# The last four rounds of a fused four-layer convolution in another order

## The chip, the cores and the metric

The kernel runs on one core of one Trainium2 chip. The metric is the device time of one execution in microseconds (us). TensorE (PE in the profile) multiplies matrices, VectorE (DVE), ScalarE (ACT) and GpSimd (POOL) work elementwise, and SyncE (SP) issues most of the transfers. Each engine takes its instructions in the order in which the program issues them to it.

## The reference

Each of 128 samples has 64 channels of 1024 positions. Four convolutions with three taps run one after the other, with weights that are modulated and normalised per sample; the second doubles the length and blurs, the fourth blurs and halves it. The input is added at the end.

```python
s = style @ mw.T + mb
weight = SCALE * w * s[:, None, :, None]
demod = lax.rsqrt(jnp.sum(weight * weight, axis=(2, 3)) + EPS)
weight = weight * demod[:, :, None, None]
...
for i, typ in enumerate(('same', 'upsample', 'same', 'downsample')):
    out = _layer(out, style, weights[i], biases[i], mod_w[i], mod_b[i], typ)
x = x + out
```

## The kernel before, in words

**What is multiplied.** The four layers of one sample are one linear map with nine taps of 64 by 64. The kernel works on quads of four samples, 32 quads in all (`q` counts from 0 to 31). For each quad TensorE first folds the layers: `stage1` (tile S), `stage2` (tile R) and `stage3` (tile Wf, in two parts), each followed by a scaled copy on ScalarE (`scaled_copy`, L361 for a copy on ScalarE). The nine taps stand in Wf as three groups a, b, c of three. Then the quad's samples, split into three planes by position modulo three, are convolved by five products instead of nine: products 0 and 4 use a and c as they are, products 1, 2 and 3 use combinations h1, h2, h3 of a, b, c (tile H).

**The work of one quad outside TensorE.**
- `combine_a` and `combine_b` (L601, L611) build h1, h3 and h2 on VectorE by `sum_of` (L595); `residual` (L587, L592) adds the identity to b.
- `in3` (L642), `in_g01` (L647), `in_g2` (L652) and `in04` (L667) make the combined planes on VectorE (tiles T and G); `in1` and `in2` (L657, L662) run on GpSimd for most quads and on VectorE for the last one.
- All five products run through `product` (L676; matmuls at L687). Products 3, 1, 2 and 0 use one pair of banks psA in that order, product 4 uses the pair Y. One group of a product is 8 matmul instructions, a whole product 24.
- Between the products the banks are read: `copy_m3` (L716, ScalarE, L719) after product 3, `sum1` (L724) after product 1, `sum2` (L733: first Y, then y at L738) after product 2. Product 1 adds into the banks that `copy_m3` reads, product 2 into those that `sum1` reads, product 0 into those that `sum2` reads, so each of them waits for the reader before it. Product 4 adds into Y and waits for the first half of `sum2`.
- `output` (L748; L756 on ScalarE, L758 on VectorE) scales a plane and adds the bias, `store` (L760) sends it to memory.

**The order.** Nothing is planned by a program: the loop at L1211 writes the order out by hand, and each engine keeps it. Round `q` holds the folding of quad `c = q + 2` (stages 2 and 3) and `s = q + 4` (stage 1), products 4 and 0 of quad `q`, and products 3, 1 and 2 of quad `n = q + 1`. On TensorE a middle round reads: stage2(c), product 4 of q, stage3(c, 0), product 3 of n, stage3(c, 1), product 0 of q group 0, product 1 of n with stage1(s) between its groups, product 0 of q groups 1 and 2 with the rest of stage1(s), product 2 of n. Rounds 28 and 29 have no stage 1 (s is 32 and more), and round 30 (L1245 to L1267) and round 31 (L1216 to L1228) have texts of their own. In round 29 VectorE also prepares quad 31: `combine_a(31)` with `sum1(30)` between its steps (L1330), `combine_b(31)`, and after `sum2(30)` its `in1` and `in2` (L1369 to L1372).

**Banks.** The psA of quads 0 to 30 come from a pool of two pairs (ps_conv). The psA of quad 31 comes at L1247 from ps_w, a pool of one pair of single banks that the folding stages use too; since these are two tiles, `copy_m3`, `sum1` and `sum2` of quad 31 work bank by bank, with two instructions each.

**The row ends** are computed apart: `slot(ends3, ...)` (L1308; matmuls at L924 into psE of ps_w, two copies at L779), `rest3` (L1014) and `rest3_bias` (L1026, and one transfer).

**EXTRA** (L1167 to L1198) hangs small steps of the scales and tables at places (round, place): place 0 before `in04(n)`, place 1 before `sum1(n)`, place 2 before product 2's second group. `var_newton` (L265, three VectorE instructions at L256 to L258) refines the inverse roots of layers i to j for quads 8 to 31; `table_C` (L305, GpSimd, L288) multiplies two of them for the R copies from quad 8 on; `small_rest` (L1159, L860 and L861) makes a bias vector on VectorE.

Of the kernel before, what the change touches and what calls it, by code (L numbers as in the profile page):

```python
# [50 lines left out]
ALU = mybir.AluOpType  # L51
# [12 lines left out]
def kernel(  # L64
# [12 lines left out]
    NQ = B // 4  # L77
# [187 lines left out]
    def var_newton(bs, ls=slice(0, NL)):  # L265

        newton(var[:, ls, bs], dm[:, ls, bs], nw[:, ls, bs])
# [37 lines left out]
    def table_C(bs, eng=nc_g):  # L305
        table(eng, tC, bs, slice(0, 2), slice(2, 4), dm[:, 1, bs], dm[:, 0, bs])

    def table_3(bs):
        table(nc_g, t3, bs, ALT, ODD, dm[:, 3, bs], var[:, 3, bs])
        table(nc_g, td, bs, slice(0, 2), slice(2, 4), dm[:, 3, bs], 1.0)  # L310
# [283 lines left out]
    def sum_of(out, x, f, y, op=ALU.add):  # L594
        nc_v.scalar_tensor_tensor(out, x, f, y, op0=ALU.mult, op1=op)  # L595
# [2 lines left out]
        W, H_ = Wq[q]  # L598
        return *(W[:, :, i] for i in range(K)), *(H_[:, i] for i in range(3))

    def combine_a(q, between=None):  # L601

        chain.pop(q)
        a, b, c, h1, h2, h3 = taps(q)
        sum_of(h1, c, -2.0, a)
        residual(q)
        if between:
            between()
        sum_of(h3, h1, 1.0 / 6.0, b)

    def combine_b(q):  # L611

        a, b, c, h1, h2, h3 = taps(q)
        sum_of(h2, c, -0.5, a)
        sum_of(h1, b, -3.0, h2, ALU.subtract)
        sum_of(h2, h2, -1.0 / 3.0, b)


    NJ = NB + 2
# [81 lines left out]
    def parts(q):  # L701

        if isinstance(A[q], list):
            return [(slice(s, s + 1), A[q][s][:, None, :NB]) for s in range(2)]
        return [(slice(0, 2), A[q][:, :, :NB])]
# [6 lines left out]
    def conv3(q, pool=None):  # L712
        A[q] = unit(pool, f"psA{q}") if pool else ps_conv.tile([P, 2, 512], F32, tag="u", name=f"psA{q}")
        product(q, 3, banks(q))
# [15 lines left out]
    def conv2(q, *groups):  # L730
        product(q, 2, banks(q), groups or range(K))

    def sum2(q):  # L733
        m3 = m3c.pop(q)
        for s, a in parts(q):
            sum_of(Y[:, s, :NB], m3[:, s], 3.0, a)
        for s, a in parts(q):
            nc_v.tensor_sub(y1w[q][:, s], y1w[q][:, s], a)  # L738

    def conv4(q, *groups):  # L740
# [31 lines left out]
    def slot(matmuls, n, ps, wide=WIDE):  # L772

        matmuls(ps)
        turn[0] ^= 1
        r = raw[turn[0]]
        for i in range(2):
            src = ps[i][:, : HB * max(n, wide)].rearrange("c (b j) -> c b j", b=HB)
            nc_a.copy(r[:, i, : HB * n].rearrange("c (b j) -> c b j", b=HB), src[:, :, :n])  # L779
# [29 lines left out]
    def vector_Da(bs):  # L809
        nc_g.tensor_mul(Da[:, bs], sc[:, 3, bs], dm[:, 2, bs])  # L810
# [5 lines left out]
    def vector_c0(bs):  # L816
        with_bias(c0f, dm[:, 1], 0, bs)
# [4 lines left out]
    def vector_c2(bs):  # L822
        with_bias(c2f, sc[:, 3], 2, bs)
# [335 lines left out]
    def small_rest(q):  # L1159
        l, bs = SMALL[q]  # L1160
        const_rest(l, bs, high(bs.stop - bs.start))

    def layers(i, j):
        return REST, slice(i, j)
# [6 lines left out]
        (3, 0): lambda: var_newton(*layers(2, 3)),  # L1171
        (3, 1): lambda: (table_A(REST, dm[:, 2, REST]), small_rest(3)),
        (3, 2): lambda: (table_b(PART[1]), table_0(REST), vector_b1(REST), tap_differences()),
        (4, 0): lambda: var_newton(*layers(0, 2)),
        (4, 2): lambda: (vector_c0(REST), table_C(REST)),
        (5, 0): lambda: var_newton(*layers(3, 4)),
        (5, 1): lambda: small_rest(5),
        (5, 2): lambda: (table_3(REST), vector_c2(REST), vector_Da(REST)),
        (6, 1): lambda: small_rest(6),
        (7, 1): lambda: small_rest(7),  # L1180
        (7, 2): lambda: (table_b(REST), zeros()),
# [11 lines left out]
        (22, 0): lambda: (blur_side(0, 0), blur_side(1, 0)),  # L1193
        (23, 0): lambda: (blur_side(0, 1), blur_side(1, 1)),
        (24, 0): lambda: (blur_side(0, 2), blur_side(1, 2)),
        (28, 2): rest3,
        (29, 0): rest3_bias,
    }  # L1198

    def extra(*at):  # L1200
# [10 lines left out]
    for q in range(NQ):  # L1211
# [32 lines left out]

        if n == NQ - 1:  # L1245

            conv3(n, ps_w)  # L1247
            copy_m3(n)
            conv4(q, 0, 1)
            for i in range(2):  # L1250
                output(q, 1, i)
            conv1(n)
            sum1(n)
            conv4(q, 2)
            for i in range(2):
                output(q, 2, i)
                store(q, i, slice(1, K))
            in04(n, PAIR[0])
            in04(n, PAIR[1])
            conv0(q, 0)  # L1260
            conv2(n)
            conv0(q, 1, 2)
            sum2(n)
            for i in range(2):
                output(q, 0, i)
                store(q, i, slice(0, 1))
            continue  # L1267
# [36 lines left out]
            stage3(c, 1)  # L1304
        if q in SLOTS:
            slot(*SLOTS[q], Y_banks)
        if q == NQ - 4:
            slot(ends3, 3, unit(ps_w, "psE"), 3)  # L1308
        conv0(q, 0)
        if q in SMALL:  # L1310
            small(q)
        if q == 2:
# [2 lines left out]
        if twice:  # L1315
            stage1(s - 1)
        elif s < NQ:
            stage1_a(s)
        conv1(n, 1, 2)
        for i in range(2):  # L1320
            output(q, 1, i)
# [2 lines left out]
        if q > 1:  # L1324
            in_g2(c)
            if not late(q):
                load(c + NX)
        extra(q, 1)
        if n == NQ - 2:
            combine_a(n + 1, lambda: sum1(n))  # L1330
            combine_b(n + 1)
        else:
            sum1(n)
        if q == 0:
            in3(c)
        if q == 1:
            in_g01(c)
        conv0(q, 1)
        if twice:
            stage1_a(s)  # L1340
        elif s < NQ:
# [25 lines left out]
            scale3(s + 2)  # L1367
        conv2(n, 1, 2)
        if n == NQ - 2:  # L1369
            sum2(n)  # L1370
            in1(n + 1, nc_v)
            in2(n + 1, nc_v)  # L1372
        for i in range(2):
            store(q, i, slice(0, 1 if late(q) else K))
# [78 lines left out]
```

## Time and profile before

| | |
|---|---|
| median of 3 runs | 482.5 us (482.35, 482.5, 485.54) |
| the profiled execution | 481.36 us, of which its span is 479.6 us |
| PE busy | 471.5 us (98%) |
| DVE busy | 397.8 us (83%) |
| ACT busy | 304.3 us (63%) |
| POOL busy | 137.8 us (29%) |
| granted TensorE clock | 0.998 |

Times in the views are us from the start of the span. In a timeline row stand the start, the time from the first start to the last end, the engine, the line, the operation, the written and the read tile, the number of instructions, and in brackets how long the engine had been idle and what released it. Ends of matmuls are modelled: the next matmul starts about 0.2 us before the end of the one before it, so that the distance between two starts says more than the length of a row.

### The profile page before, as it was taken

The numbers are of one execution on the slowest core, as the hardware profiler recorded it, in microseconds if no ns is written. First come the engines' busy times: TensorE is split into PE (matmuls) and PEld (weight loads), VectorE is DVE, ScalarE is ACT, GpSimd is POOL, SyncE is SP. The second block draws the span as 40 slices with busy tenths as digits, with TensorE's granted clock in tenths as the row PEclk, the third lists the DMA queues.
The fourth block names the chain that finished last, engine by engine and source line by source line (L and its number), as shares of the span: only waits on it lengthen the run. The fifth ranks groups of instructions, "written<-read, shape, count | busy, mean of one in ns | idle before, by whom it ended". The sixth has DMA issues, their size and how long they took to land. (4 is left out here: it accounts for less than half of the span.)

```text
span 479.6 us, 25784 instructions
## 1 busy us (share of the span) xinstructions
PE 471.5 (98%) x11592; PEld 356.3 (74%) x11592; DVE 397.8 (83%) x660; ACT 304.3 (63%) x621; POOL 137.8 (29%) x171
## 2 busy tenths in 40 slices
PE   8999999999999999999999999999999999999996
PEld 7977788878788877777777777666777777777753
DVE  4899998798898988878868988758988887787784
ACT  5465666666666766767667666667666666765442
POOL 3433132644314333303333212333113333322100
PEclk9999999999999999999999999999999999999999
DMA  7116365245444535443445544444543445554314
GB/s 248 55 56 208 105 203 182 91 150 178 151 151 123 169 126 180 149 150 111 160 150 160 168 149 142 135 143 155 166 150 123 154 152 180 162 164 150 106 62 176
DMA packets 50494, 70.65 MB, mean 147 GB/s; under 512 B 5648, under 2 KB 47312, under 8 KB 50384
## 3 DMA queue, kind: packets, MB, share of 16 engines
q1 hardware_dynamic: 49792, 68.32, 44.3%
q8 instruction: 91, 1.49, 1.3%
q10 hardware_dynamic: 592, 0.69, 0.4%
q14 instruction: 19, 0.16, 0.1%
HBM read 35.36 MB, written 33.62 MB: 144 GB/s over the span
## 5 line engine op out<-in xcount | busy, mean ns | idle before, releaser
L687 PE MATMUL psA<-T,H 64*64 64x340 f32 x2304 | 190.8, 446 | 1.2 <-DVE y L595 1.2
L687 PEld LDWEIGHTS psA<-T,H 64*64 64x64 f32 x2304 | 93.5, 133 | 52.9 <-issue 3.4
L446 POOL TENSOR_TENSOR S<-S 128x128 f32<-128x128 f32 x28 | 14.3, 511 | 268.8 <-ACT S L361 259.9
L595 DVE SCALAR_TENSOR_TENSOR G<-X 128x684 f32<-128x684 f32 (+1 forms) x65 | 76.5, 1212 | 0.0
L687 PE MATMUL psA<-T,Wf 64*64 64x340 f32 x768 | 74.0, 446 | 0.0
L361 ACT ACTIVATE R<-psR,tC 128x448 f32<-128x448 f32 x63 | 36.6, 631 | 42.4 <-PE psR L467 26.6
L361 ACT ACTIVATE Wf<-psW,t 128x384 f32<-128x384 f32 (+1 forms) x126 | 56.4, 498 | 11.1 <-PE psW L574 10.2
L687 PE MATMUL Y<-T,Wf 64*64 64x340 f32 x768 | 61.7, 446 | 0.1
L574 PE MATMUL psW<-R,w0s 64*64 64x128 f32 (+1 forms) x1536 | 61.7, 287 | 0.0
L574 PEld LDWEIGHTS psW<-R,w0s 64*64 64x64 f32 x1536 | 51.2, 133 | 6.9
L595 DVE SCALAR_TENSOR_TENSOR Y<-m,psA 128x680 f32<-128x680 f32 (+1 forms) x33 | 28.0, 849 | 33.3 <-PE psA L687 32.8
L665 POOL TENSOR_TENSOR T<-G 128x684 f32<-128x684 f32 x28 | 50.7, 1811 | 0.0
L674 DVE TENSOR_TENSOR T<-G 128x1368 f32<-128x1368 f32 (+1 forms) x33 | 50.6, 1537 | 0.1
L660 POOL TENSOR_TENSOR T<-G 128x684 f32<-128x684 f32 x28 | 46.5, 1659 | 14.0 <-DVE G L595 14.0
L595 DVE SCALAR_TENSOR_TENSOR y<-psA,m 128x680 f32<-128x680 f32 (+1 forms) x33 | 27.8, 844 | 25.3 <-PE psA L687 24.7
L756 ACT ACTIVATE o<-Y,tb,td 128x340 f32<-128x340 f32 x63 | 36.6, 631 | 18.5 <-PE Y L687 15.9
L467 PE MATMUL psR<-S,E 64*64 64x64 f32 (+1 forms) x1536 | 48.3, 237 | 0.0
L390 PEld LDWEIGHTS psS<-wd,w2n 64*64 64x64 f32 x1120 | 36.9, 133 | 11.0 <-issue 0.3
L467 PEld LDWEIGHTS psR<-S,E 64*64 64x64 f32 x1536 | 40.4, 134 | 5.7
L756 ACT ACTIVATE o<-psA,tb,td 128x340 f32<-128x340 f32 x63 | 37.0, 646 | 8.2 <-PE psA L687 8.2
L687 PEld LDWEIGHTS Y<-T,Wf 64*64 64x64 f32 x768 | 30.6, 133 | 15.1 <-issue 0.6
L361 ACT ACTIVATE S<-psS,tBn 128x256 f32<-128x256 f32 x56 | 23.5, 471 | 28.5 <-PE psS L390 28.5
(153 smaller groups left out, 693.0 us busy)
## 6 DMA issues: line engine op xcount, KB each, us to landing
out<-o SPq DMA_DIRECT2D x167, 170.0 KB, 2.6
X<-in_x SPq DMA_DIRECT2D x150, 172.0 KB, 3.3
X<-in_x SPq DMA_DIRECT2D x14, 516.0 KB, 4.9
out<-o SPq DMA_DIRECT2D x6, 510.0 KB, 5.2
out<-o SPq DMA_DIRECT2D x2, 340.0 KB, 2.7
Xe<-in_x_ends SPq DMA_DIRECT2D x1, 512.0 KB, 6.4
out<-o ACTq DMA_DIRECT2D x3, 170.0 KB, 3.2
par<-in_params SPq DMA_DIRECT2D x2, 192.0 KB, 3.5
```

What stands on the lines that cost most here:

```text
L361: nc_a.activation(dst, src, AF.Copy, scale=f)
L390: nc.tensor.matmul(ps[r][cols, at * C : (at + n) * C], weight[rows], wd[c if r == 0 else 1 - c][rows, taps], start=first, stop=last, skip_ ...
L446: nc_g.tensor_add(t[:, :, 2], t[:, :, 2], t[:, :, 0])
L467: nc.tensor.matmul(dst[r][cols], weight[rows], st[c if r == 0 else 1 - c][rows, slots, :], start=False, stop=last, skip_group_check=True,)
L574: nc.tensor.matmul(ps[r][cols, at : at + m * C], w0s[kind][rows, k, :], rt[c][rows, first : first + K * (m - 1) + 1 : K, :], start=(n == 1 ...
L595: nc_v.scalar_tensor_tensor(out, x, f, y, op0=ALU.mult, op1=op)
L660: eng.tensor_add(t[:, :, 0, :NJ], plane(g, 2), plane(g, 1))
L665: eng.tensor_sub(t[:, :, 1, :NJ], plane(g, 2), plane(g, 1))
L674: nc_v.tensor_sub(t[:, pairs, :, :NJ], both(a, PL), both(b, 1))
L687: nc.tensor.matmul(ps[s][cols, :NB], w, Ts[q, tag][rows, c, i, g : g + NB], start=(g == 0 and m == 3), stop=(g == K - 1), skip_group_check ...
L756: nc_a.activation(dst, src, AF.Identity, bias=add, scale=d3)
```

## The change

Eight edits, all in the order of the program. No matmul is added or removed.

1. In rounds 28 and 29 group 0 of product 0 of q no longer stands before product 1 of n; groups 0 and 1 stand together after `sum1(n)`.
2. The row ends' `ends3` goes, in round 28, from before product 0's group 0 to behind group 0 of product 1.
3. `rest3` moves from place (28, 2) to (28, 1), ahead of `sum1(29)` on VectorE, and `rest3_bias` from (29, 0) to (28, 2).
4. In round 29 `sum1(30)` comes first, then all of `combine_a(31)` and the first step of `combine_b(31)`; before, h1 and the residual of quad 31 stood ahead of `sum1(30)`.
5. After product 2 of quad 30 the steps on VectorE are interleaved: Y of `sum2(30)`, second step of `combine_b(31)`, `in1(31)`, y of `sum2(30)`, third step of `combine_b(31)`, `in2(31)`.
6. The psA of quad 31 comes from ps_conv, as one tile.
7. `var_newton` for layers 0 and 1 at (4, 0) is split: layer 1 stays, layer 0 goes to (5, 0), ahead of layer 3's. So there are three calls of 96 columns instead of one of 192 and one of 96.
8. `table_C` goes from (4, 2) to (5, 2), where it stands on GpSimd behind `in1(7)` and `in2(7)`, and `small_rest(5)` from (5, 1) to (5, 2).

```diff
@@ -598,22 +598,20 @@
         W, H_ = Wq[q]
         return *(W[:, :, i] for i in range(K)), *(H_[:, i] for i in range(3))
 
-    def combine_a(q, between=None):
+    def combine_a(q):
 
         chain.pop(q)
         a, b, c, h1, h2, h3 = taps(q)
         sum_of(h1, c, -2.0, a)
         residual(q)
-        if between:
-            between()
         sum_of(h3, h1, 1.0 / 6.0, b)
 
-    def combine_b(q):
+    def combine_b(q, steps=range(3)):
 
         a, b, c, h1, h2, h3 = taps(q)
-        sum_of(h2, c, -0.5, a)
-        sum_of(h1, b, -3.0, h2, ALU.subtract)
-        sum_of(h2, h2, -1.0 / 3.0, b)
+        plan = (h2, c, -0.5, a), (h1, b, -3.0, h2, ALU.subtract), (h2, h2, -1.0 / 3.0, b)
+        for i in steps:
+            sum_of(*plan[i])
 
 
     NJ = NB + 2
@@ -730,11 +728,10 @@
     def conv2(q, *groups):
         product(q, 2, banks(q), groups or range(K))
 
-    def sum2(q):
-        m3 = m3c.pop(q)
-        for s, a in parts(q):
-            sum_of(Y[:, s, :NB], m3[:, s], 3.0, a)
-        for s, a in parts(q):
+    def sum2(q, steps=(0, 1)):
+        for s, a in parts(q) if 0 in steps else ():
+            sum_of(Y[:, s, :NB], m3c.pop(q)[:, s], 3.0, a)
+        for s, a in parts(q) if 1 in steps else ():
             nc_v.tensor_sub(y1w[q][:, s], y1w[q][:, s], a)
 
     def conv4(q, *groups):
@@ -1171,11 +1168,10 @@
         (3, 0): lambda: var_newton(*layers(2, 3)),
         (3, 1): lambda: (table_A(REST, dm[:, 2, REST]), small_rest(3)),
         (3, 2): lambda: (table_b(PART[1]), table_0(REST), vector_b1(REST), tap_differences()),
-        (4, 0): lambda: var_newton(*layers(0, 2)),
-        (4, 2): lambda: (vector_c0(REST), table_C(REST)),
-        (5, 0): lambda: var_newton(*layers(3, 4)),
-        (5, 1): lambda: small_rest(5),
-        (5, 2): lambda: (table_3(REST), vector_c2(REST), vector_Da(REST)),
+        (4, 0): lambda: var_newton(*layers(1, 2)),
+        (4, 2): lambda: vector_c0(REST),
+        (5, 0): lambda: (var_newton(*layers(0, 1)), var_newton(*layers(3, 4))),
+        (5, 2): lambda: (table_C(REST), small_rest(5), table_3(REST), vector_c2(REST), vector_Da(REST)),
         (6, 1): lambda: small_rest(6),
         (7, 1): lambda: small_rest(7),
         (7, 2): lambda: (table_b(REST), zeros()),
@@ -1193,8 +1189,8 @@
         (22, 0): lambda: (blur_side(0, 0), blur_side(1, 0)),
         (23, 0): lambda: (blur_side(0, 1), blur_side(1, 1)),
         (24, 0): lambda: (blur_side(0, 2), blur_side(1, 2)),
-        (28, 2): rest3,
-        (29, 0): rest3_bias,
+        (28, 1): rest3,
+        (28, 2): rest3_bias,
     }
 
     def extra(*at):
@@ -1244,7 +1240,7 @@
 
         if n == NQ - 1:
 
-            conv3(n, ps_w)
+            conv3(n)
             copy_m3(n)
             conv4(q, 0, 1)
             for i in range(2):
@@ -1304,9 +1300,8 @@
             stage3(c, 1)
         if q in SLOTS:
             slot(*SLOTS[q], Y_banks)
-        if q == NQ - 4:
-            slot(ends3, 3, unit(ps_w, "psE"), 3)
-        conv0(q, 0)
+        if s < NQ:
+            conv0(q, 0)
         if q in SMALL:
             small(q)
         if q == 2:
@@ -1316,6 +1311,8 @@
             stage1(s - 1)
         elif s < NQ:
             stage1_a(s)
+        elif q == NQ - 4:
+            slot(ends3, 3, unit(ps_w, "psE"), 3)
         conv1(n, 1, 2)
         for i in range(2):
             output(q, 1, i)
@@ -1326,16 +1323,15 @@
             if not late(q):
                 load(c + NX)
         extra(q, 1)
+        sum1(n)
         if n == NQ - 2:
-            combine_a(n + 1, lambda: sum1(n))
-            combine_b(n + 1)
-        else:
-            sum1(n)
+            combine_a(n + 1)
+            combine_b(n + 1, (0,))
         if q == 0:
             in3(c)
         if q == 1:
             in_g01(c)
-        conv0(q, 1)
+        conv0(q, *((1,) if s < NQ else (0, 1)))
         if twice:
             stage1_a(s)
         elif s < NQ:
@@ -1367,8 +1363,11 @@
             scale3(s + 2)
         conv2(n, 1, 2)
         if n == NQ - 2:
-            sum2(n)
+            sum2(n, (0,))
+            combine_b(n + 1, (1,))
             in1(n + 1, nc_v)
+            sum2(n, (1,))
+            combine_b(n + 1, (2,))
             in2(n + 1, nc_v)
         for i in range(2):
             store(q, i, slice(0, 1 if late(q) else K))
```

## The prediction

> **What bounds the kernel now.** I read the page's head first, then the waits of TensorE, then the timelines of the last four rounds engine by engine, and last the two early rounds in which edits 7 and 8 lie. The head of the page, and the largest of the waits but one at the start (us in total, times, longest):
>
> ```profile
> span 479.6 us, 25784 instructions
> PE 471.5 (98%) x11592; PEld 356.3 (74%) x11592; DVE 397.8 (83%) x660; ACT 304.3 (63%) x621; POOL 137.8 (29%) x171
> ```
>
> ```profile
> PE psA L687 <- DVE y L595: 1.2, 3, 0.8
> ```
>
> TensorE is the bound; its idle time is 8.1 us with start and end. The change takes no matmul away, so it can only win waits, and those are few. The listed idle is too small: it is counted from a modelled end, while the next matmul normally starts before that end. I therefore measure by starts. TensorE in rounds 28 to 31:
>
> ```profile
> 439.41 0.97 PE L574 MATMUL psW<-R,w0s 64*64 64x128 f32 x24
> 440.86 1.69 PE L924 MATMUL psE<-Ue,par 64*64 64x192 f32 x22 [0.48 <-ACT Wf L361]
> 442.60 0.48 PE L687 MATMUL psA<-T,Wf 64*64 64x340 f32 x4
> ...
> 444.88 1.34 PE L687 MATMUL psA<-T,Wf 64*64 64x340 f32 x14
> 446.20 1.95 PE L687 MATMUL psA<-T,H 64*64 64x340 f32 x24
> ...
> 456.15 0.78 PE L687 MATMUL psA<-T,Wf 64*64 64x340 f32 x8
> 456.72 1.92 PE L687 MATMUL psA<-T,H 64*64 64x340 f32 x24
> 458.44 1.35 PE L687 MATMUL psA<-T,Wf 64*64 64x340 f32 x16
> 460.56 3.66 PE L687 MATMUL psA<-T,H 64*64 64x340 f32 x48 [0.77 <-DVE y L595]
> ...
> 465.16 1.92 PE L687 MATMUL psA<-T,H 64*64 64x340 f32 x24
> 466.88 0.78 PE L687 MATMUL Y<-T,Wf 64*64 64x340 f32 x8
> ...
> 469.73 1.50 PE L687 MATMUL psA<-T,Wf 64*64 64x340 f32 x16
> 471.31 1.95 PE L687 MATMUL Y<-T,Wf 64*64 64x340 f32 x24
> 473.05 1.92 PE L687 MATMUL psA<-T,Wf 64*64 64x340 f32 x24
> ```
>
> From start to start a product of 24 takes 1.72 (465.16 to 466.88), so a group of 8 takes 0.57 and 16 take 1.14; the row's 1.92 reaches 0.20 beyond the next start. The 24 of a second part of stage 3 take 0.97 less that overhang, 0.77. Against that pitch four gaps stand out. Round 28: psE could start at 439.41 + 0.77 = 440.18 and starts at 440.86, **0.68**; product 2 of quad 29 could start at 444.88 + 1.00 and starts at 446.20, **0.32**. Round 29: product 2 of quad 30 could start at 458.44 + 1.14 = 459.58 and starts at 460.56, **0.98**. Round 30: the last product 4 could start at 469.73 + 1.14 = 470.87 and starts at 471.31, **0.44**. Together 2.42 us. VectorE and ScalarE in the same rounds say why:
>
> ```profile
> 452.87 1.24 DVE L1026 SCALAR_TENSOR_TENSOR Oe<-Oe,par_s,Xe 64x384 f32<-64x384 f32 x2
> ...
> 456.42 2.37 DVE L595 SCALAR_TENSOR_TENSOR G<-X 128x1376 f32<-128x1376 f32 x2
> ...
> 459.56 0.86 DVE L595 SCALAR_TENSOR_TENSOR y<-psA,m 128x680 f32<-128x680 f32 x1
> ...
> 470.02 1.14 DVE L595 SCALAR_TENSOR_TENSOR Y<-m,psA 128x340 f32<-128x340 f32 x2 [0.35 <-issue]
> ```
>
> ```profile
> 439.67 0.73 ACT L719 COPY m<-psA 128x680 f32<-128x680 f32 x1 [0.71 <-PE psA L687]
> 440.39 0.73 ACT L361 ACTIVATE Wf<-psW,t 128x192 f32<-128x192 f32 x2
> 442.52 0.63 ACT L779 COPY raw<-psE 128x192 f32<-128x192 f32 x2 [1.40 <-PE psE L924]
> ...
> 455.71 0.73 ACT L719 COPY m<-psA 128x680 f32<-128x680 f32 x1 [0.75 <-PE psA L687]
> ...
> 459.85 1.16 ACT L756 ACTIVATE o<-psA,tb,td 128x340 f32<-128x340 f32 x2 [1.61 <-PE psA L687]
> ```
>
> psE stands in the banks that the Wf copies of 440.39 still read. In round 29 VectorE is late: Oe (the ends' bias, 1.24) and quad 31's first two steps (from the end of G at 458.79 to 459.56, 0.77) stand ahead of `sum1(30)`, which starts at 459.56 although product 1 ended at 456.72 + 1.92 = 458.64. It ends at 460.42, and TensorE goes on at 460.56: 0.14 from the end on VectorE to the matmul, which I use for ScalarE too. In round 30 Y takes two instructions, 1.14, because the banks are two tiles.
>
> **The change, part by part** (times in the clock of the profile before; the chain of starts is the sum).
>
> Round 28, edits 1, 2, 3. Product 1 of quad 29 now follows stage 3 directly, and so meets the copy of product 3, which product 0's group 0 and psE used to cover: 439.67 + 0.73 + 0.14 = 440.54 instead of 440.18, a new wait of 0.36. Its group 0 ends at 441.11, and psE follows without a wait (the second Wf copy ends at 441.12 and the second bank's first matmul comes four instructions later). psE takes 442.60 - 440.86 = 1.74, to 442.85; groups 1 and 2 of product 1 to 443.99, product 0 whole (1.72) to 445.71. `sum1(29)` stands behind `rest3` on VectorE, which waits for the raw copies (some 443.1 to 443.7); the row of 442.52 gives 0.63 for them, `rest3` ends near 444.3, `sum1(29)` 0.87 later, plus 0.14 makes 445.3, below 445.71. The 0.32 is gone, since 24 matmuls lie over `sum1` instead of 16. `rest3_bias` and its transfer then run in VectorE's idle time before `sum2(29)`; SP takes the transfer between stores and nothing waits for it. Product 2 of quad 29 starts at 445.71 instead of 446.20: **-0.49**.
>
> Round 29, edits 1, 3, 4. Stage 3 ends at 456.15 - 0.49 = 455.66; the copy of product 3 ends at 455.71 - 0.49 + 0.73 = 455.95, so product 1 of quad 30 starts at 456.09: a new wait of 0.43, where there was none. It ends its issue at 457.81, product 0 of quad 29 at 459.53. VectorE is free at 458.79 - 0.49 - 1.24 (Oe gone) = 457.06, so `sum1(30)` now waits for TensorE, starts near 458.05 and frees the banks at 459.06: hidden. Product 2 of quad 30 starts at 459.53 instead of 460.56: **-1.03**. What is late next is the copy of product 3.
>
> Round 30, edits 5, 6. Product 3 of quad 31 comes at 461.25 and now needs the bank pair of quad 29, which the two outputs of the row of 459.85 read: shifted, 459.79 + 1.16 + 0.14 = 461.09, so 0.16 to spare; h3 (some five steps of VectorE after 458.05) near 460.5. Product 4's first groups at 462.97 need Y, ready at 462.5; product 1 of quad 31 at 464.11 needs `in1`, which stands behind Y and one step (0.6) and ends near 463.6, and the copy of product 3, 461.25 + 1.92 + 0.08 + 0.73 + 0.14 = 464.12, even. It then goes to 465.84, product 4's last group to 466.41, product 0's to 466.98. `sum1(31)` is one instruction, done at 467.10: a wait of 0.12. Product 2 goes to 468.82, product 0 of quad 30 to 469.96; Y, now one instruction of 0.87, is done at 470.08: a wait of 0.12 instead of 0.44. Product 4 takes 1.74 (471.31 to 473.05), so the last product starts at 471.82 instead of 473.05. **Tail: -1.23.** All behind it (outputs, last stores) is as before. Bounds: -1.0 if the spare 0.16 and the even copy turn into waits, -1.5 if the copies release 0.1 sooner each.
>
> Edits 7 and 8. Rounds 4 and 5 on TensorE, VectorE, GpSimd and ScalarE:
>
> ```profile
> 100.83 0.79 PE L687 MATMUL psA<-T,Wf 64*64 64x340 f32 x7
> 101.87 1.95 PE L687 MATMUL psA<-T,H 64*64 64x340 f32 x24 [0.25 <-DVE y L595]
> ...
> 115.97 1.93 PE L687 MATMUL psA<-T,H 64*64 64x340 f32 x24
> ```
>
> ```profile
> 94.59 0.61 DVE L256 TENSOR_TENSOR nw<-dm,var 128x192 f32<-128x192 f32 x1
> ...
> 95.76 0.36 DVE L258 SCALAR_TENSOR_TENSOR dm<-nw,dm 128x192 f32<-128x192 f32 x1
> 96.04 1.57 DVE L674 TENSOR_TENSOR T<-G 128x1368 f32<-128x1368 f32 x1
> ...
> 108.53 0.25 DVE L256 TENSOR_TENSOR nw<-dm,var 128x96 f32<-128x96 f32 x1
> ...
> 109.39 0.14 DVE L1297 MEMSET Y<- 128x96 f32 x1
> ...
> 113.98 0.25 DVE L860 TENSOR_TENSOR cc<-Y,a 128x96 f32<-128x96 f32 x1
> ...
> 114.60 0.87 DVE L595 SCALAR_TENSOR_TENSOR y<-psA,m 128x680 f32<-128x680 f32 x1
> ```
>
> ```profile
> 94.94 0.57 POOL L458 TENSOR_TENSOR Ed<-E 128x128 f32<-128x128 f32 x1
> ...
> 104.80 0.68 POOL L288 TENSOR_TENSOR tC<-dm 64x48 f32<-64x48 f32 x2
> ...
> 116.40 1.83 POOL L665 TENSOR_TENSOR T<-G 128x684 f32<-128x684 f32 x1
> ```
>
> ```profile
> 119.95 1.16 ACT L361 ACTIVATE R<-psR,tC 128x448 f32<-128x448 f32 x2 [1.09 <-PE psR L467]
> ```
>
> In round 4 product 2 of quad 5 could start at 100.83 + 0.5 = 101.36 and starts at 101.87, behind `sum1(5)`: 0.51 to win. Ahead of it VectorE spends 94.59 to 96.04 = 1.45 on the refinement of 192 columns. Three instructions of 96 columns take 0.86 where nothing else runs (108.53 to 109.39), which would save 0.59 and win all 0.51. But in round 4 they lie beside GpSimd's Ed until 95.51: the first took 0.61, the third, behind it, 0.36. With the second held until 95.51, as it is now, and a third of some 0.26 the refinement ends near 95.85, saving 0.2. I take **-0.2**, from the row with the same neighbours; ends 0 and -0.51. The Trainium skill, page "SBUF — State Buffer", section "SBUF: two separate sides", says that VectorE with two SBUF inputs and GpSimd lock a shared pair of ports for a whole instruction, the other blocking; by that rule the early term is -0.2 (sum -1.43), without it -0.51 (sum -1.74). The 0.61 against 0.36 for the same 192 columns speak for it.
>
> Round 5 gets a second refinement, +0.86, and loses `small_rest` ahead of `sum1(6)`, 114.60 - 113.98 = 0.62: `sum1(6)` is 0.24 later against TensorE. It freed its banks at 115.47 + 0.14 for a start at 115.97, 0.36 to spare: nothing. `small_rest(5)` goes into VectorE's idle time behind it. `table_C` on GpSimd now ends near 116.40 + 1.83 + 0.68 = 118.9, and the R copy needs it at 119.95: nothing.
>
> **Sum:** -1.23 - 0.2 = -1.43 against the profiled execution: 481.36 to 479.9. That execution lies 1.14 below the median of 482.5, so the median after is forecast at 482.5 - 1.4 = **481.1 us**.
>
> **The rivals.** (a) The early edit wins its full 0.51 and the two new copy waits are shorter than I make them: -1.74 to -2.4, 480.1 to 480.8. Speaks for it that 0.86 stands in a row; against it the held row of 94.59. (b) The tail gives half: product 3 of quad 31 in the shared pair has only 0.16 to spare, and were ScalarE's outputs of quad 29 late by one more pair (1.16), TensorE would wait 1.00 there, leaving -0.43: 482.1. Against it: ScalarE idled 1.61 ahead of the row of 459.85. (c) Slower: `table_C`, put behind two long GpSimd instructions, is late for R of quad 8. It has 1.05 to spare and R's copy then delays stage 3; it must be 1.05 + 1.43 = 2.5 us later than reckoned to make the kernel slower, which the two at 1.83 each do not do unless they take nearly twice as long. At 3.4 us late it costs 2.35: 482.5 + 0.9 = 483.4. (d) The edits only move the waits to the copies of product 3: those are counted with 0.36 and 0.43; at 1.0 each the tail would give nothing, 482.3.
>
> **How the numbers follow.** My forecast (-1.0 to -1.9) 0.68, (a) 0.14, (b) and (d) together 0.15, (c) 0.03. The range takes (a) from the profiled execution's side, 481.36 - 2.1 = 479.3, and on the other side no gain, 482.5. A measurement of this kernel can tell about 1% (4.8 us) from no change: its own runs span 3.2 us. All cases but odd runs lie within that: faster 0.02, same 0.96, slower 0.02.
>
> **What would show it.** Right: no wait of psE, none of product 2 for `sum1(30)`; two short waits of product 1 for `copy_m3` in rounds 28 and 29; Oe ahead of `sum2(29)`; the last product 1.2 to 1.9 earlier in the span; the gap in round 4 smaller than 0.51 but not gone. Wrong: a wait of product 3 of quad 31 for an output, a wait of R of quad 8 for tC, or a new gap in round 5 ahead of product 2.

## The result, and the profile after

| | before | after |
|---|---|---|
| median, 20 runs each | 482.62 us (481.21 to 485.54) | 481.72 us (480.93 to 483.55) |
| ratio of the times, 95% interval | | 0.9986, 0.9974 to 0.9999 |
| the profiled execution, its span | 481.36, 479.6 us | 482.28, 480.4 us |

The kernel is 0.14% faster, 0.7 us with an interval of 0.05 to 1.25: the sign was forecast, the 1.43 us are not in the interval, and by the classes of the forecast it is "same". The two profiles do not show it in their spans, since the profiled execution lies 1.26 below the median before and 0.56 above the median after. They have to be compared stretch by stretch. The table gives starts of TensorE's matmuls (us from the start of the span) and what lies between them, for the two kernels.

| | before | after | difference |
|---|---|---|---|
| product 4 of quad 4 starts (round 4) | 91.08 | 91.07 | -0.01 |
| from there to product 4 of quad 5 | 14.46 | 13.93 | **-0.53** |
| from there to product 4 of quad 28 (rounds 5 to 27) | 328.92 | 330.35 | +1.43 |
| from there to product 2 of quad 29 | 11.74 | 11.95 | **+0.21** |
| from there to product 2 of quad 30 | 14.36 | 13.79 | **-0.57** |
| from there to the last product | 12.49 | 12.32 | **-0.17** |

Where the program was changed it wins 0.53 early and 0.53 in the tail (the last three rows), 1.06 together. The 1.43 lie in rounds whose program is the same but for round 5, which took 14.08 in both; they are taken up with the last experiments. Behind the start of the last product the profile after is another 0.44 longer (6.99 against 6.55 to the end of the span); the two other profiles of the kernel before have 7.84 and 6.31 there, so this differs from execution to execution. TensorE in rounds 28 to 31 of the kernel after:

```profile
440.35 0.98 PE L574 MATMUL psW<-R,w0s 64*64 64x128 f32 x24
441.43 0.80 PE L685 MATMUL psA<-T,H 64*64 64x340 f32 x8
442.02 1.70 PE L921 MATMUL psE<-Ue,par 64*64 64x192 f32 x24
443.43 1.45 PE L685 MATMUL psA<-T,H 64*64 64x340 f32 x16
444.58 2.01 PE L685 MATMUL psA<-T,Wf 64*64 64x340 f32 x24
447.30 1.95 PE L685 MATMUL psA<-T,H 64*64 64x340 f32 x24 [0.71 <-DVE y L595]
...
456.49 0.97 PE L574 MATMUL psW<-R,w0s 64*64 64x128 f32 x24
457.64 1.95 PE L685 MATMUL psA<-T,H 64*64 64x340 f32 x24 [0.17 <-issue]
459.37 1.92 PE L685 MATMUL psA<-T,Wf 64*64 64x340 f32 x24
461.09 3.64 PE L685 MATMUL psA<-T,H 64*64 64x340 f32 x48
...
470.40 1.32 PE L685 MATMUL psA<-T,Wf 64*64 64x340 f32 x16
471.65 1.95 PE L685 MATMUL Y<-T,Wf 64*64 64x340 f32 x24
```

The wait of psE is gone, and so are the 0.98 ahead of product 2 of quad 30 (459.37 + 1.72 = 461.09, no gap) and three quarters of the 0.44 ahead of the last product 4 (470.40 + 1.14 = 471.54, then 0.11). The two waits for `copy_m3` are there: 441.43 against 440.35 + 0.77 = 441.12, and 457.64 against 457.26. But product 2 of quad 29 could start at 444.58 + 1.72 = 446.30 and starts at 447.30: a new gap of 1.00. VectorE and GpSimd at that place, first a timeline, then the single instruction in it that a narrower window picks out:

```profile
444.01 2.37 DVE L1011 SCALAR_TENSOR_TENSOR Oe<-raw,dm 128x192 f32<-128x192 f32 x2 [1.40 <-ACT raw L776]
446.30 0.85 DVE L595 SCALAR_TENSOR_TENSOR y<-psA,m 128x680 f32<-128x680 f32 x1
```

```profile
444.58 1.80 DVE L1011 SCALAR_TENSOR_TENSOR Oe<-raw,dm 128x192 f32<-128x192 f32 x1
```

```profile
442.79 1.66 POOL L658 TENSOR_TENSOR T<-G 128x684 f32<-128x684 f32 x1 [9.45 <-DVE G L595]
444.39 1.77 POOL L663 TENSOR_TENSOR T<-G 128x684 f32<-128x684 f32 x1
```

`rest3` multiplies raw by dm, both in SBUF. Its second instruction took 1.80 us and ended at 446.38, 0.22 after `in2(30)` on GpSimd (444.39 + 1.77 = 446.16). `sum1(29)` stands behind it and came at 446.30, although its product 1 had ended at 444.88. In the profile before, `rest3` ran after `in2(30)` had ended (at 445.51), and both instructions together took 0.61:

```profile
445.97 0.61 DVE L1014 SCALAR_TENSOR_TENSOR Oe<-raw,dm 128x192 f32<-128x192 f32 x2
```

Round 4 of the kernel after, VectorE, GpSimd and TensorE:

```profile
94.56 0.51 DVE L256 TENSOR_TENSOR nw<-dm,var 128x96 f32<-128x96 f32 x1
95.10 0.40 DVE L257 SCALAR_TENSOR_TENSOR nw<-nw,dm 128x96 f32<-128x96 f32 x1
95.53 0.26 DVE L258 SCALAR_TENSOR_TENSOR dm<-nw,dm 128x96 f32<-128x96 f32 x1
95.71 1.58 DVE L672 TENSOR_TENSOR T<-G 128x1368 f32<-128x1368 f32 x1
...
97.98 2.36 DVE L595 SCALAR_TENSOR_TENSOR G<-X 128x1376 f32<-128x1376 f32 x2
100.26 0.86 DVE L595 SCALAR_TENSOR_TENSOR y<-psA,m 128x680 f32<-128x680 f32 x1
```

```profile
94.92 0.46 POOL L458 TENSOR_TENSOR Ed<-E 128x128 f32<-128x128 f32 x1
99.63 1.03 POOL L446 TENSOR_TENSOR S<-S 128x128 f32<-128x128 f32 x1 [4.25 <-ACT S L361]
```

```profile
101.36 1.97 PE L685 MATMUL psA<-T,H 64*64 64x340 f32 x24
```

The same place before, where the two differ:

```profile
98.31 2.63 DVE L595 SCALAR_TENSOR_TENSOR G<-X 128x1376 f32<-128x1376 f32 x2
```

```profile
99.64 0.57 POOL L446 TENSOR_TENSOR S<-S 128x128 f32<-128x128 f32 x1 [4.13 <-ACT S L361]
```

The gap is gone: 101.36 is the start that the profile before allowed (the group's first matmul stands at 100.79, one ahead of the row of 100.83, and 100.79 + 0.57 = 101.36). The roots, from 94.56 to 95.71, took 1.15 instead of 1.45, and GpSimd's Ed still held the first two (0.51 and 0.40 against 0.25 and 0.26 undisturbed). The other 0.27 come from G: before, GpSimd's add at 99.64 came between the two G instructions and VectorE waited; now VectorE is 0.3 earlier, has its second G going, and GpSimd waits (1.03 instead of 0.57).

### The profile page after: what moved, and what is told of

Same layout as the page of the kernel before. It is cut to its first block, busy times and chain, and to the rows that moved or that the text cites. A ratio compares the mean times of both kernels' runs of the same rounds, so it can differ in the third digit from the quotient of the medians.

```text
span 480.4 us, 25778 instructions
## 1 busy us (share of the span) xinstructions
PE 472.2 (98%) x11592; PEld 369.2 (77%) x11592; DVE 399.0 (83%) x660; ACT 303.8 (63%) x620; POOL 138.9 (29%) x171
## 4 chain that ended last, share of the span: by engine, by line
PE 97%; DVE 2%; issue 0%; ACT 0%; ACTq 0%; DVEq 0%
PE psA L685 45%; PE psW L574 15%; PE Y L685 11%; PE psR L467 10%; PE psS L390 6%; PE psR L533 4%; PE psA L467 2%; PE Y L921 2%; PE Y L337 1%; PE Y L181 1%; DVE Oe L1011 0%; PE psM L205 0%; DVE o L755 0%; DVE y L595 0%; PE psE L921 0%
## 5 line engine op out<-in xcount | busy, mean ns | idle before, releaser
L685 PE MATMUL psA<-T,H 64*64 64x340 f32 x2304 | 193.3, 446 | 1.2 <-DVE y L595 0.9
L685 PEld LDWEIGHTS psA<-T,H 64*64 64x64 f32 x2304 | 100.2, 133 | 46.6 <-issue 3.3
L574 PE MATMUL psW<-R,w0s 64*64 64x128 f32 (+1 forms) x1536 | 63.1, 287 | 0.0
L574 PEld LDWEIGHTS psW<-R,w0s 64*64 64x64 f32 x1536 | 53.2, 133 | 5.9
L595 DVE SCALAR_TENSOR_TENSOR Y<-m,psA 128x680 f32<-128x680 f32 x32 | 27.8, 870 | 33.3 <-PE psA L685 33.3
L467 PE MATMUL psR<-S,E 64*64 64x64 f32 (+1 forms) x1536 | 50.6, 237 | 0.2 <-issue 0.2
L467 PEld LDWEIGHTS psR<-S,E 64*64 64x64 f32 x1536 | 43.2, 134 | 5.1 <-issue 0.3
L595 DVE SCALAR_TENSOR_TENSOR y<-psA,m 128x680 f32<-128x680 f32 x32 | 27.7, 865 | 23.1 <-PE psA L685 20.6
L390 PEld LDWEIGHTS psS<-wd,w2n 64*64 64x64 f32 x1120 | 38.3, 133 | 9.5
L685 PEld LDWEIGHTS Y<-T,Wf 64*64 64x64 f32 x768 | 32.9, 133 | 13.9 <-issue 1.1
```

The lines of the kernel that those rows point to most:

```text
L390: nc.tensor.matmul(ps[r][cols, at * C : (at + n) * C], weight[rows], wd[c if r == 0 else 1 - c][rows, taps], start=first, stop=last, skip_ ...
L467: nc.tensor.matmul(dst[r][cols], weight[rows], st[c if r == 0 else 1 - c][rows, slots, :], start=False, stop=last, skip_group_check=True,)
L574: nc.tensor.matmul(ps[r][cols, at : at + m * C], w0s[kind][rows, k, :], rt[c][rows, first : first + K * (m - 1) + 1 : K, :], start=(n == 1 ...
L685: nc.tensor.matmul(ps[s][cols, :NB], w, Ts[q, tag][rows, c, i, g : g + NB], start=(g == 0 and m == 3), stop=(g == K - 1), skip_group_check ...
```

## The experiments

My theory after the result: **VectorE's instructions with two SBUF inputs and GpSimd's instructions exclude each other, and whoever starts second waits to the other's end.** It makes `rest3` late in round 28 (a loss of 1.0), and in round 4 it makes a small lead into a larger one. The rivals: the reordering around product 1 itself costs the time in round 28, and the number of columns alone sets the length of the roots in round 4. In the edits, lines that start with a minus are the kernel named, those with a plus the experiment.

All runs in one table, by the starts of the profiles. Round 4 is from product 4 of quad 4 to that of quad 5, round 28 from product 4 of quad 28 to that of quad 29, the tail from product 4 of quad 28 to the last product.

| kernel | round 4 | round 28 | tail | rounds 5 to 27 |
|---|---|---|---|---|
| before | 14.46 | 15.98 | 38.59 | 328.92 |
| after | 13.93 | 16.19 | 38.06 | 330.35 |
| e1, rest3 behind sum1 | 13.93 | 15.12 | 37.08 | 329.04 |
| e2, rest3 with a PSUM operand | 13.94 | 15.12 | 37.08 | 329.19 |
| e3, edits 7 and 8 alone | 13.94 | 16.03 | 38.63 | 329.72 |
| e4, Ed a round earlier alone | 13.93 | 16.01 | 38.62 | 329.26 |
| e5, e1 with other fillers | 13.94 | 14.82 | 36.51 | 330.59 |
| e6, e1 without edit 6 | 13.93 | 15.15 | 37.25 | 329.56 |
| e7, e1 without edit 5 | 13.94 | 15.15 | 37.60 | 329.35 |
| e8, e3 with small_rest in its old place | 13.93 | 16.03 | 38.63 | 329.63 |
| e9, rest3 moved alone | 14.44 | 16.35 | 38.96 | 329.29 |
| e10, after again | 13.93 | 16.24 | 38.11 | 329.62 |
| before, second profile | 14.44 | 16.00 | 38.60 | 329.05 |
| before, third profile | 14.44 | 16.03 | 38.64 | 329.40 |

The stretches repeat within 0.05 us from profile to profile of one kernel, rounds 5 to 27 within 0.8. Differences of 0.1 us in the changed rounds can be read from one profile each. Only e1, e3 and e5 were timed twelve times; the other experiments ran once, and of them only the starts are used.

**e1: `rest3` back behind `sum1(29)`.** Against the kernel after:

```diff
-        (28, 1): rest3,
-        (28, 2): rest3_bias,
+        (28, 2): lambda: (rest3(), rest3_bias()),
```

> The changed kernel with rest3 put back behind sum1(29), ahead of rest3_bias; nothing else. Theory (port): in the changed kernel the second instruction of rest3, which reads two SBUF tensors, stood still from 444.58 until GpSimd's in2(30) ended at 446.16, and sum1(29) behind it came 1.3 us late. Then here sum1(29) follows product 1 at once, the gap ahead of product 2 of quad 29 falls from 1.00 to under 0.1 us, the tail is some 1.0 us shorter than in the changed kernel and the whole about 1.7 us (0.35%) faster than before. Rival: the round is late because product 1 and the row ends' matmuls were reordered around the copy of product 3; then sum1(29) still ends late, a gap of 0.5 us or more stays in round 28 and the time is that of the changed kernel, 0.14% under before.

TensorE, then VectorE in round 28 of this kernel:

```profile
442.89 2.02 PE L685 MATMUL psA<-T,Wf 64*64 64x340 f32 x24
444.61 2.02 PE L685 MATMUL psA<-T,H 64*64 64x340 f32 x24
```

```profile
443.31 0.87 DVE L595 SCALAR_TENSOR_TENSOR y<-psA,m 128x680 f32<-128x680 f32 x1 [1.98 <-PE psA L685]
444.10 1.16 DVE L1011 SCALAR_TENSOR_TENSOR Oe<-raw,dm 128x192 f32<-128x192 f32 x2
```

No gap is left ahead of product 2 (444.61 - 442.89 = 1.72), round 28 is 1.07 shorter than after, the tail 0.98. `rest3` is still held (1.16 instead of 0.61), but nothing that matters stands behind it. Measured: 481.23 us against 482.19, ratio 0.9977 (0.9965 to 0.9989), 1.1 us with an interval of 0.5 to 1.7; the forecast of 0.35% is at its edge. By its time alone it cannot be told from the kernel after, by its starts it can. The rival falls, since product 1 keeps its new order here.

**e2: one of `rest3`'s operands from PSUM.** Same place and same copies as in the kernel after; `psE` keeps the two banks. The kernel leaves out the fourth layer's roots for the row ends, so what it computes there is not the reference's; it serves for the times alone.

```diff
+    psE = []
...
-                spread(dm[:, 3, bs], 3),
+                psE[h][:, : 3 * HB].rearrange("c (b j) -> c b j", j=3),
...
-            slot(ends3, 3, unit(ps_w, "psE"), 3)
+            psE.extend(unit(ps_w, "psE"))
+            slot(ends3, 3, psE, 3)
```

> The changed kernel with rest3 in its new place, behind the same copies, but its second operand is read from PSUM (the row ends' own bank) instead of the table of inverse roots in SBUF, so it has one SBUF input; the row ends are therefore scaled by themselves instead of the fourth layer's roots. Theory (port): with one SBUF input nothing holds it while GpSimd runs in1(30) and in2(30): two instructions of about 0.35 us, 0.6 to 0.7 together instead of 2.37, and the gap ahead of product 2 of quad 29 falls from 1.00 to under 0.1. Rival: rest3 is long because of what it waits for or where it stands (its copies, its strided operand): then it still takes 2 us or more and the gap stays near 1.0.

VectorE and GpSimd in round 28:

```profile
443.26 0.62 DVE L1013 SCALAR_TENSOR_TENSOR Oe<-raw,psE 128x192 f32<-128x192 f32 x2 [0.99 <-ACT raw L776]
444.18 0.87 DVE L595 SCALAR_TENSOR_TENSOR y<-psA,m 128x680 f32<-128x680 f32 x1 [0.30 <-PE psA L685]
444.96 1.79 DVE L1025 SCALAR_TENSOR_TENSOR Oe<-Oe,par_s,Xe 64x384 f32<-64x384 f32 x2
```

```profile
442.44 1.66 POOL L658 TENSOR_TENSOR T<-G 128x684 f32<-128x684 f32 x1 [9.45 <-DVE G L595]
444.05 1.66 POOL L663 TENSOR_TENSOR T<-G 128x684 f32<-128x684 f32 x1
```

With GpSimd running beside it from 442.44 to 445.71 the pair took 0.62, no longer than undisturbed, and VectorE was idle for 0.30 before `sum1(29)`. Round 28 is that of e1. `rest3_bias`, which has two SBUF inputs, took 1.79 instead of 1.24 in the same run. So it is the operand that decides, not the place or the copies. The new operand also has another stride; but with the old stride, and GpSimd idle, the pair took 0.61 in the profile before.

**e3: edits 7 and 8 alone, on the kernel before.**

```diff
-        (4, 0): lambda: var_newton(*layers(0, 2)),
-        (4, 2): lambda: (vector_c0(REST), table_C(REST)),
-        (5, 0): lambda: var_newton(*layers(3, 4)),
-        (5, 1): lambda: small_rest(5),
-        (5, 2): lambda: (table_3(REST), vector_c2(REST), vector_Da(REST)),
+        (4, 0): lambda: var_newton(*layers(1, 2)),
+        (4, 2): lambda: vector_c0(REST),
+        (5, 0): lambda: (var_newton(*layers(0, 1)), var_newton(*layers(3, 4))),
+        (5, 2): lambda: (table_C(REST), small_rest(5), table_3(REST), vector_c2(REST), vector_Da(REST)),
```

> The kernel before with edits 7 and 8 alone (inverse roots split; table_C and small_rest(5) moved). If the two ends of the change add up: the gap ahead of product 2 of quad 5 goes from 0.51 to under 0.1, no new gap in rounds 5 and 6, the last four rounds as before, and the time 0.5 us (0.1%) below before. On record I took 0.2 for it. Rival: what the changed kernel shows in round 4 hangs on something else than these edits, and the gap stays at 0.3 to 0.5.

Round 4 went from 14.46 to 13.94, rounds 5 and 6 kept 14.08 and 14.09, the tail stayed (38.63). Measured: 481.76 us against 482.19, ratio 0.9989 (0.9975 to 1.0003): the 0.5 us lie in the interval, but so does no gain at all. By the starts, edits 7 and 8 alone win in round 4 what they win in the whole change.

**e4: GpSimd's Ed a round earlier, on the kernel before.** VectorE's program is untouched.

```diff
-        (2, 2): lambda: (table_B(REST), table_Bn(REST), vector_a1(REST)),
+        (2, 2): lambda: (table_B(REST), table_Bn(REST), vector_a1(REST), tap_differences()),
...
-        (3, 2): lambda: (table_b(PART[1]), table_0(REST), vector_b1(REST), tap_differences()),
+        (3, 2): lambda: (table_b(PART[1]), table_0(REST), vector_b1(REST)),
```

> The kernel before with only GpSimd's tap differences (Ed) moved a round earlier, from place (3, 2) to (2, 2); VectorE's program is the same to the last instruction, the roots are not split. Theory (port): the three instructions of 192 columns in round 4 are no longer held and take about 0.36 to 0.4 each, some 1.15 us in all instead of 1.45; in_g2 then reaches the port before GpSimd's add at L446, which now waits instead of it (0.27 more); sum1(5) comes 0.5 earlier and the gap ahead of product 2 of quad 5 falls from 0.51 to under 0.15. Rival: the columns alone set the length; then the three still take 1.4 us and the gap stays at 0.5.

VectorE in round 4:

```profile
93.98 0.34 DVE L256 TENSOR_TENSOR nw<-dm,var 128x192 f32<-128x192 f32 x1
94.36 0.36 DVE L257 SCALAR_TENSOR_TENSOR nw<-nw,dm 128x192 f32<-128x192 f32 x1
94.75 0.36 DVE L258 SCALAR_TENSOR_TENSOR dm<-nw,dm 128x192 f32<-128x192 f32 x1
95.03 1.58 DVE L674 TENSOR_TENSOR T<-G 128x1368 f32<-128x1368 f32 x1
```

All 192 columns in 1.05 us, shorter than the 1.15 that the changed kernel needs for 96, and round 4 is 13.93: moving three instructions of GpSimd wins the whole gap without the split. The rival, that the columns alone set the length, falls. GpSimd's add then took 0.67, 0.10 more than before and not the 0.27 more that I expected.

**e5: other fillers, on e1.** Group 0 of product 0 back over the copy of product 3, the row ends' matmuls over `sum1(29)`.

```diff
-        if s < NQ:
-            conv0(q, 0)
+        conv0(q, 0)
...
-        elif q == NQ - 4:
-            slot(ends3, 3, unit(ps_w, "psE"), 3)
         conv1(n, 1, 2)
+        if q == NQ - 4:
+            slot(ends3, 3, unit(ps_w, "psE"), 3)
...
-        conv0(q, *((1,) if s < NQ else (0, 1)))
+        conv0(q, 1)
```

> The kernel of the first experiment with other fillers in rounds 28 and 29: product 0's group 0 stands before product 1 again, over the copy of product 3, the row ends' matmuls stand behind product 1, over sum1, and product 0's groups 1 and 2 stay behind. If the waits of product 1 for the copy (0.32 in round 28, 0.47 in round 29 by starts in that run) are what is left: both go; in round 29 only 16 matmuls lie over sum1(30), 1.14 against about 1.35 from the last start of product 1 to its banks being free, so a new wait of about 0.2 ahead of product 2 of quad 30. Round 28 0.3 and round 29 0.25 shorter, from product 4 of quad 28 to the last product 36.5 instead of 37.08 us, and the time some 0.5 us below the first experiment's. Rival: the order around product 1 costs as much as it wins, and the tail stays at 37.1.

TensorE in rounds 28 and 29:

```profile
441.30 0.79 PE L685 MATMUL psA<-T,Wf 64*64 64x340 f32 x8
441.87 1.93 PE L685 MATMUL psA<-T,H 64*64 64x340 f32 x24
443.59 1.62 PE L921 MATMUL psE<-Ue,par 64*64 64x192 f32 x24
444.99 1.37 PE L685 MATMUL psA<-T,Wf 64*64 64x340 f32 x16
446.14 1.94 PE L685 MATMUL psA<-T,H 64*64 64x340 f32 x24
...
456.07 0.79 PE L685 MATMUL psA<-T,Wf 64*64 64x340 f32 x8
456.64 1.94 PE L685 MATMUL psA<-T,H 64*64 64x340 f32 x24
458.35 1.37 PE L685 MATMUL psA<-T,Wf 64*64 64x340 f32 x16
459.70 3.66 PE L685 MATMUL psA<-T,H 64*64 64x340 f32 x48
```

Both waits for the copy are gone (441.30 + 0.57 = 441.87, and 456.07 + 0.57 = 456.64), the new wait ahead of product 2 of quad 30 is 459.70 - 458.35 - 1.14 = 0.21, and the tail is 36.51, as forecast. Measured: 480.50 us against 482.72, ratio 0.9963 (0.9948 to 0.9979). It beats the kernel before. That it also beats the kernel after, with which it was not timed side by side, rests on its starts, by which it is the best of all; its interval and that of the change (0.9974 to 0.9999) overlap only from 0.9974 to 0.9979.

**e6: edit 6 undone, on e1** (quad 31 in the single banks).

```diff
-            conv3(n)
+            conv3(n, ps_w)
...
-            sum_of(Y[:, s, :NB], m3c.pop(q)[:, s], 3.0, a)
+            sum_of(Y[:, s, :NB], m3c[q][:, s], 3.0, a)
```

> The kernel of the first experiment with edit 6 undone: quad 31's psA from the single banks again. By my step on Y (one instruction of 0.87 instead of two of 1.14 in all): the gap ahead of the last product 4 goes from about 0.1 back to 0.4, the rest stays, and the stretch from product 4 of quad 28 to the last product is 0.3 longer, 37.4. Rival: Y's gap hung on VectorE being late in round 30, not on the banks; then it stays at 0.1.

```profile
467.99 1.50 PE L685 MATMUL psA<-T,Wf 64*64 64x340 f32 x16
469.57 1.95 PE L685 MATMUL Y<-T,Wf 64*64 64x340 f32 x24
```

The gap ahead of the last product 4 is 469.57 - 467.99 - 1.14 = 0.44 again, as expected. The tail grew by 0.17 only: with single banks the 0.11 ahead of product 2 of quad 31 are not there. Edit 6 is worth 0.17.

**e7: edit 5 undone, on e1** (no interleaving).

```diff
-            combine_b(n + 1, (0,))
+            combine_b(n + 1)
...
-            sum2(n, (0,))
-            combine_b(n + 1, (1,))
-            in1(n + 1, nc_v)
-            sum2(n, (1,))
-            combine_b(n + 1, (2,))
-            in2(n + 1, nc_v)
+            sum2(n)
+            in1(n + 1, nc_v)
+            in2(n + 1, nc_v)
```

> The kernel of the first experiment with edit 5 undone: all of combine_b(31) before sum2(30), then both halves of sum2(30), then in1 and in2. VectorE has 0.58 us idle ahead of Y in that run, which takes one of the two steps; Y comes 0.1 to 0.6 later and product 4 has about 0.6 to spare, in1 ends earlier against product 1 of quad 31. I expect no change: 37.1 from product 4 of quad 28 to the last product, within 0.1. Rival: Y late by more than its slack, a gap of some 0.3 ahead of product 4 of quad 30.

```profile
462.58 1.37 PE L685 MATMUL Y<-T,Wf 64*64 64x340 f32 x16
464.22 1.95 PE L685 MATMUL psA<-T,H 64*64 64x340 f32 x24 [0.26 <-DVE T L658]
```

My expectation failed: product 1 of quad 31 waits 464.22 - 462.58 - 1.14 = 0.50 for `in1(31)`, and the tail is 0.52 longer. I had put `in1` earlier; it comes later. Counted from product 4 of quad 28 it starts at 28.84 instead of 27.99 in e1: Y starts 0.55 later, because both steps of `combine_b(31)` now stand ahead of it, and the 0.77 of y take the place of a step of 0.47. Edit 5 is worth 0.5.

**e8: the split without moving `small_rest(5)`**, on e3.

```diff
-        (5, 2): lambda: (table_C(REST), small_rest(5), table_3(REST), vector_c2(REST), vector_Da(REST)),
+        (5, 1): lambda: small_rest(5),
+        (5, 2): lambda: (table_C(REST), table_3(REST), vector_c2(REST), vector_Da(REST)),
```

> The kernel before with the roots split and table_C moved, but small_rest(5) left at (5, 1) ahead of sum1(6). The gap in round 4 goes as in the third experiment (0.51 to under 0.05). In round 5 VectorE has 0.86 more ahead of sum1(6) and nothing less, against 0.36 to spare: a new gap of 0.5 ahead of product 2 of quad 6, so that the starts from there on stand where they stood before the change. Rival: GpSimd's add at L446 or the port takes part as in round 4 and the gap is 0.2 or less, or 0.75 and more.

Round 4 is 13.93, and the next round, from product 4 of quad 5 to that of quad 6, grew from 14.08 to 14.35: a gap of 0.27, about half of what I expected. In its profile the two refinements take 1.60 together (107.11 to 108.71), 0.74 more than the one before and not 0.86, and `sum1(6)` starts 0.18 after the start of `small_rest`'s last instruction instead of 0.34. Counted from product 4 of quad 5, `sum1(6)` starts at 9.68 instead of 9.06: 0.62 later, against 0.36 to spare. So half of the split's gain hangs on moving `small_rest`.

**e9: `rest3` moved alone, on the kernel before.**

```diff
-        (28, 2): rest3,
+        (28, 1): rest3,
```

> The kernel before with one instruction pair moved: rest3 from place (28, 2) to (28, 1), ahead of sum1(29). Theory (port): rest3 meets in1(30) and in2(30) on GpSimd (442.25 to 445.51 in the profile before); its second instruction ends some 0.2 us after in2, sum1(29) follows at about 445.7 instead of 445.19, and the gap ahead of product 2 of quad 29 grows from 0.32 to 0.7 to 0.9; round 28 from 15.98 to about 16.4 us. Rival: in the changed kernel it was the later row-end matmuls that made rest3 late; here they come early, so rest3 is done by 443.7, and round 28 stays at 15.98.

VectorE and GpSimd in round 28:

```profile
443.30 2.73 DVE L1014 SCALAR_TENSOR_TENSOR Oe<-raw,dm 128x192 f32<-128x192 f32 x2 [1.03 <-ACT raw L779]
```

```profile
444.05 1.77 POOL L665 TENSOR_TENSOR T<-G 128x684 f32<-128x684 f32 x1
```

The pair ends at 446.03, 0.21 after `in2(30)` (445.82), and round 28 is 16.35 instead of 15.98, as the theory said; the gap ahead of product 2 of quad 29 grew from 0.32 to 0.65, a little less than expected.

**e10 and the kernel before twice more: rounds 5 to 27.** Nothing edited.

> The changed kernel once more, nothing edited. If the 1.4 us that rounds 5 to 27 were longer in its profile than in the one before (330.35 against 328.92 us between product 4 of quads 5 and 28) belong to the execution and not to the program, they are spread otherwise here, over other rounds and another sum, while the last four rounds (38.06 us from product 4 of quad 28 to the last product) and round 4 (13.93) repeat within 0.1. Rival: they belong to the program, and the same rounds are again longer by the same amounts.

> The kernel before once more, nothing edited. In two profiles of the changed kernel rounds 5 to 27 took 330.35 and 329.62 us, against 328.92 in the one profile before, and round 27 took 14.28 and 14.31 against 13.94. If these extra times belong to the execution, this profile of the kernel before shows some too: 329.0 to 330.5 for rounds 5 to 27. Rival: they came with the change; then it repeats 328.9 and 13.94. Round 4 (14.46) and the last four rounds (38.59) repeat within 0.1 by either.

> The kernel before a third time, for the same question: by the one theory rounds 5 to 27 lie anywhere between 328.9 and 330.5 us, by the other at 328.9 as in the first profile.

The tail and round 4 repeat (table). Rounds 5 to 27 took 330.35 and 329.62 after, 328.92, 329.05 and 329.40 before. In the third profile before, the rounds of quads 26 and 27 took 14.08 and 14.19 instead of 13.94; in the two after, quad 27's took 14.28 and 14.31, and round 19 took 17.15 in one and the usual 16.54 in the other. The second execution before, 485.98 us long, lost its time elsewhere: product 4 of quad 4 started at 94.27 instead of 91.08. So such extra times occur without the change and differ from execution to execution, and most of the 1.43 belong to the execution. The program of rounds 5 to 27 is that of the kernel after in e1, e2, e3, e5, e6 and e7 too, and that of the kernel before in e4 and e9. The eight profiles of the first kind took 329.04 to 330.59, the middle one 329.59, the five of the second 328.92 to 329.40, the middle one 329.26. The ranges overlap, and the long round 27 also occurs in e3 (14.27), which has the last four rounds of the kernel before; but that some 0.3 us come with the change is not excluded. It would make the 1.06 of the starts into the 0.7 of the times. In the profile after, the stops in these rounds show as idle time of TensorE that the trace puts down to nothing ("issue"); I did not find their cause.

## Why the prediction was right or wrong

- **Right in class and sign, too large in size.** 481.1 was forecast, 481.72 measured, inside the range; of the 1.43 the starts show 1.06 and the times 0.7 (0.05 to 1.25). That the sum of the starts comes so near is in part luck: the tail gave 0.70 less than forecast and round 4 0.33 more. One sign that I had named did not come: the last product starts at 473.41, not 1.2 to 1.9 earlier than at 473.05, since rounds 5 to 27 hide the gain. The 1% that I held a measurement could tell from no change was too coarse: with 20 runs each the interval is 0.25% wide.
- **Round 28, the step that failed:** "`rest3` ends near 444.3, `sum1(29)` 0.87 later". I took 0.6 for `rest3` from the profile before, in which it ran behind `in2(30)`, and did not look at what GpSimd does at the new place. There it runs `in1(30)` and `in2(30)` for 3.4 us. The round's first stretch was to be 0.49 shorter and became 0.21 longer; e1, e2 and e9 show that `rest3`'s second SBUF operand is the whole of it. The Trainium skill, page "SBUF — State Buffer", section "SBUF: two separate sides", states the rule (an exclusive lock for a whole instruction, "the other fully blocks"), and the trace agrees: the ends lie 0.22 and 0.21 behind GpSimd's. I had used that rule for round 4 and not for round 28, where the change itself puts such an instruction on the path.
- **A size off in the same step, hidden by the failure:** I gave psE 1.74, its distance to the row of 442.60 in the profile before; two matmuls of product 0 stand ahead of that row, at 442.30. It takes 442.02 to 443.43 = 1.41. Before, it had still waited inside for its second bank: two of its matmuls started at 440.86, the next at 441.13, when the second Wf copy had ended at 441.12. Without `rest3` the stretch to product 2 of quad 29 is 444.61 - 433.70 = 10.91 in e1 (product 4 of quad 28 started at 433.70), 0.83 shorter than before, not 0.49.
- **Round 29, right:** -0.54 forecast, -0.57 measured; the wait for the copy 0.38 instead of 0.43, `sum1(30)` hidden. In round 28 this wait was 0.31 instead of 0.36. The 0.14 that I took from VectorE for ScalarE was too much: product 1 starts 0.09 and 0.11 after the end of the copy.
- **Round 30, right:** -0.20 forecast, -0.17 measured. Product 3 of quad 31 did not wait for an output. What edits 5 and 6 are worth, e7 and e6 show: 0.5 and 0.17.
- **Round 4, the mechanism half right, the size wrong:** I took 0.2 and it gave 0.53. The roots themselves won 0.30, about as reckoned under the lock; I left out that the same lock stands 3.6 us further on, between G and GpSimd's add, and that a lead of 0.3 turns it round. e4 gets the same 0.53 by moving GpSimd's work alone.
- **Round 5, right:** the second refinement cost nothing. The moved `small_rest` did meet GpSimd:

```profile
116.73 1.42 DVE L858 SCALAR_TENSOR_TENSOR cc<-b1s,cc 128x96 f32<-128x96 f32 x1
118.08 0.86 DVE L595 SCALAR_TENSOR_TENSOR Y<-m,psA 128x680 f32<-128x680 f32 x1
```

  In the kernel after its second instruction took 1.42 instead of 0.26, ending 0.11 after `in2(7)` on GpSimd (116.19 + 1.85 = 118.04), and held Y back to 118.08, which was just not too late: product 4 of quad 6 started at 119.08, with 14.08 from the one before, as in the profile before.
- **The rivals:** (a) came true in its early half (0.53 for 0.51), while the two copy waits were only 0.05 shorter each; e1, with `rest3` back behind `sum1(29)`, has the tail at -1.51 instead of -1.23. Of (b) the outcome came, a tail of less than half, but not its wait for an output. (c) and (d) did not occur. The loss came by a way that I had not listed.

## What to carry to other kernels

An instruction of VectorE with two SBUF inputs can last as long as what GpSimd has running beside it (1.80 us here, where the undisturbed pair took 0.61); before such a step is moved ahead of one that TensorE waits for, look at GpSimd's rows at the new place, not at the step's own length at the old one. An operand in PSUM, or the place behind the critical instruction, takes the wait off the path. Gaps of a busy TensorE are read from start to start, and where executions differ by more than the change, stretch by stretch.

## What the hardware showed that was not expected

Between two GpSimd instructions VectorE gets one in: `rest3`'s first instruction ran from 444.01 to 444.65 across the border of `in1(30)` and `in2(30)` at 444.4, the second then waited for the whole of `in2(30)`. In e9 the first ended at 444.31, 0.21 after `in1(30)`, and the second at 446.03, 0.21 after `in2(30)`. And a lead of 0.3 us decides which of the two engines waits: GpSimd's add lasted 0.57 in the one order and 1.03 in the other, VectorE's G pair 2.63 and 2.36.
